# Attention with a sum of tanh over 128 features: the sixteen leftover keys of each image packed into three matmul banks and summed by TensorE, with smaller VectorE steps and longer rests in the side work

## The chip, the cores and the metric

The kernel runs on one core of one Trainium2 chip. The metric is the device time of one execution in microseconds; the number before is the median of three runs. All data are float32.

## The reference

The input is a batch of eight images, 128 channels of 36 x 36 points. Layer 0 is a convolutional attention block (3x3 convolutions for queries, keys and values, softmax attention over 34 x 34 key positions, a tanh, a 1x1 convolution), added to its input. Layer 1 reads each image as 1296 tokens of 128 features. Its attention scores are not a dot product:

```python
def _L1_attn_ref(x, mask, Wq, bq, Wk, bk, w, bw):
    q = jnp.einsum('bld,ed->ble', x, Wq) + bq
    k = jnp.einsum('bld,ed->ble', x, Wk) + bk
    t = jnp.tanh(q[:, :, None, :] + k[:, None, :, :])
    scores = jnp.einsum('bijd,d->bij', t, w) + bw[0]
    attn = jax.nn.softmax(scores, axis=-1)
    return jnp.einsum('bij,bjd->bid', attn, x)
...
t = t + _L1_attn_ref(_ln_t(t), ...)
t = t + _L1_ffn_ref(_ln_t(t), ...)
```

After it comes a layer of 64 experts. A softmax over the 1296 tokens gates each expert; each expert takes its eight best tokens, pools them, and writes its result back to them.

## The kernel before

**How tanh becomes matmuls.** The 128 features are split into 16 groups of five and 8 groups of six. Within a group, the sum of w tanh(q + k) is one fraction: the denominator is a sum over all sign patterns of exp(sign . q) exp(sign . k), and the numerator is the same sum with each pattern weighted by its sum of w. A group of five has 32 patterns and a group of six has 64, so a matmul over 32 or 64 rows makes one group's denominator (or numerator) for 128 keys and 432 queries. The features of the signs lie in NF = 8 blocks of 128 rows: blocks 0 to 3 hold four groups of five each, blocks 4 to 7 two groups of six each. The keys' part is `kf`, the queries' part `qf` (part 0 for denominators, part 1 for numerators).

**Units and slots.** Eight images (b), three chunks of 432 queries (c), and eleven tiles of keys (j): ten of 128 keys and a last one of REM = 16 keys. A unit is one (b, c, j); the last keys stand sixth in a chunk (`order.insert(5, NKT - 1)`). A unit of 128 keys has 12 slots, each with two groups: in turn two slots of fives from one block and one slot of sixes. The unit of the last keys has three slots (`REM_SLOTS`, L61), 2952 slots in all.

**What a slot does** (the loop at L991, in the order of the engines' queues):

```python
            take_turns(p)
            ns = numerators(p)
            denominators(p + LAG)
            terms(p, ns)
            if pending and pending[0][0] <= p:
                exps(p, *pending.popleft()[1:])
            ...
            matmul_turn(p)
            if last:
                pending.append((p + 7, u, sums(u)))
```

`denominators` runs LAG = 3 slots ahead: two matmuls into a PSUM tile `d` of two banks (two such tiles), then ScalarE takes the logarithm into `lq` (L872); every second slot one exponential with scale -1 over two slots turns the logarithms into reciprocals (L875). `numerators` makes two matmuls into two banks `n`, out of a ring of four. `terms` lets VectorE multiply numerators by reciprocals. In slots 2, 5, 8 and 11 (`DVE_PAIRS`) VectorE also adds the products up itself (L892 to L899); in the other eight the products `rp` (three buffers) go to GpSimd, which adds them to `accp` (L908, L910). `sums` (L914) adds the halves on GpSimd, and seven slots later ScalarE takes the exponential (L935) as attention weight `e`.

**The last keys before.** In a slot of the last keys (L853 to L859) four blocks stand side by side, each in 108 columns of a bank, and the four 108-query pieces of the chunk in the four 32-partition strips; the 16 keys are stored twice to fill a strip. A slot has 32 matmuls of 108 columns for the denominators and as many for the numerators. Three logarithms, two exponentials, six multiplications, two GpSimd additions of 864 columns and three more in `sums` follow.

**Side work.** Everything else is written as Python generators in four lanes: first_of_all (query blocks), urgent (the weighted sum `attend`), gates (the experts' gates of the image before), background (all of the next image: `normal`, `conv_keys`, `layer0`, `tokens`, `keys`). A generator says at each yield whether its next part wants matmuls (`matmuls(rest)`) or other engines (`TAKE`, `step(rest)`) and for how many slots it rests. `take_turns` (L958) issues one waiting part of each lane at the start of a slot, ahead of that slot's terms. `matmul_turn` (L963) issues matmuls at its end, with a budget of PACE = 350 columns per slot. The side work uses the same ring of four `n` banks. Engines run their queues in order, so a part that waits holds up whatever stands behind it.

In `tokens` (L539) each image is turned into tokens (tpl), VectorE takes the statistics of eleven tiles (L573, L574), GpSimd raises the variance to -1/2 (`rsqrt`, L221), VectorE normalizes into `xh` out of a second set of transposes (tpn, L593), and a third (tpc) makes `xT`. `keys` (L617) makes the keys' exponentials `ks` and stores them in DRAM (`kd`), from which `prefetch` loads `kf` two units ahead. In `gate_tokens` (L759) ScalarE scales the gates `probs` (L774) and VectorE finds the eight best (L777).

Of the kernel before, what the change touches and what calls it, by code (L numbers as in the profile page):

```python
# [19 lines left out]
CH = 432  # L20
# [37 lines left out]
DVE_PAIRS = (2, 5, 8, 11)  # L58
PACE = 350

REM_SLOTS = [([q + m for m in range(NF // 2)], rows) for q, rows in SLOTS[:3]]  # L61


@with_exitstack
def kernel(
# [55 lines left out]
    with ExitStack() as loop, ExitStack() as score:  # L121
# [34 lines left out]
        def load_x(b):  # L156
# [382 lines left out]
        def tokens(b):  # L539
# [42 lines left out]
            nc.gpsimd.memset(xh[:, :, C : C + 1], 1.0)  # L582
            yield matmuls()
            for g in range(0, NKT, 4):
                tp = aux("tpn")
                some = list(range(g, min(g + 4, NKT)))
                for t in some:
                    o, n = KT[t]
                    turned_to(tp[:n, (t - g) * C : (t - g + 1) * C], r[:, o : o + n], ident)
                yield TAKE  # L590
                for t in some:
                    n = KT[t][1]
                    nc.vector.tensor_scalar(  # L593
                        xh[:n, t, :C], tp[:n, (t - g) * C : (t - g + 1) * C],
                        mv[:n, t, 0:1], rs[:n, t : t + 1], ALU.subtract, ALU.mult,
                    )
                yield matmuls()
# [105 lines left out]
        def gate_logits(b, chunks):  # L703
# [23 lines left out]
            for c in chunks:  # L727
                tp, tt = turned(c, "t2T")
                yield TAKE
                nc.vector.tensor_copy(tt, tp[:, :CH])  # L730
                nc.sync.dma_start(t2d[b][:, c * CH : (c + 1) * CH], tt)
                yield matmuls(1)
                tp = aux("tp3")
                for j in range(TPC):
                    turned_to(tp[:T, j * C : (j + 1) * C], tt[:, j * T : (j + 1) * T], ident)
                yield TAKE
                for j in range(TPC):
                    t = c * TPC + j
                    nc.vector.tensor_scalar(
                        t2[:T, t, :], tp[:T, j * C : (j + 1) * C],  # L740
                        mv[:, t, 0:1], rs[:, t - tiles[0] : t - tiles[0] + 1],
                        ALU.subtract, ALU.mult,
                    )
                yield matmuls(1)
            for c in chunks:
# [13 lines left out]
        def gate_tokens(b):  # L759
# [13 lines left out]
            yield step()  # L773
            nc.scalar.activation(pr, pr, AF.Copy, scale=inv)  # L774
            yield step(2)
            top = small.tile([E, 8], F32, tag="top", name="top")
# [45 lines left out]

        def ends(u, k):

            return k % 2 == 1 or (units[u][2] == NKT - 1 and k == len(REM_SLOTS) - 1)

        def prefetch(u):
# [15 lines left out]
        def products(u, k, part, outs):  # L843
# [3 lines left out]
            if j < NKT - 1:  # L847
# [4 lines left out]
                return  # L852
            blocks, rows = REM_SLOTS[k]  # L853
            for i, q in enumerate(blocks):
                for h in range(2):
                    for s in range(TPC):
                        mm(outs[h][32 * s : 32 * s + 32, i * T : (i + 1) * T], kf[rows[h], q, :32],  # L857
                           qf_of[b, c, q][rows[h], part, s * T : (s + 1) * T],
                           start=True, stop=True)  # L859

        def denominators(p):
# [4 lines left out]
            d = ps_d.tile([128, 2, 512], F32, tag="d", name="d")  # L866
            products(u, k, 0, [d[:, h, :] for h in range(2)])
# [4 lines left out]
            nc.scalar.activation(lq[:, o : o + 2, :], d[:, :, :CH], AF.Ln)  # L872
            if ends(u, k):
                some = lq[:, : o + 2, :]
                nc.scalar.activation(some, some, AF.Exp, scale=-1.0)  # L875

        def numerators(p):
            ns = [ps_n.tile([128, 512], F32, tag="n", name="n") for _ in range(2)]
            products(*slots[p], 1, ns)
            return [ps[:, :CH] for ps in ns]  # L880

        def terms(p, ns):
# [17 lines left out]
            else:  # L900
                rp = rpp.tile([128, 2, CH], F32, tag="rp", name="rp")
                for h in range(2):
                    mult(rp[:, h, :], ns[h], lq[:, o + h, :])  # L903
                if k == 0:
                    live["r"] = rp
# [3 lines left out]
                else:  # L909
                    nc.gpsimd.tensor_add(live["p"], live["p"], rp)  # L910
            if ends(u, k):
                lq_of.pop((u, k // 2))

        def sums(u):  # L914

            s = live.pop("p")
            nc.gpsimd.tensor_add(s[:, 0, :], s[:, 0, :], s[:, 1, :])  # L917
            if units[u][2] < NKT - 1:
                d = live.pop("d")
                nc.gpsimd.tensor_add(d, s[:, 0, :], d)  # L920
                return d
            d = s[:, 0, :T]
            nc.gpsimd.tensor_add(s[:, 0, : 2 * T], s[:, 0, : 2 * T], s[:, 0, 2 * T :])
            nc.gpsimd.tensor_add(d, d, s[:, 0, T : 2 * T])
            return d
# [3 lines left out]
        def exps(p, u, d):  # L929
# [7 lines left out]
            if len(es[b, c]) == NKT:  # L937
                urgent.append(attend(b, c, es.pop((b, c))))

        class Lane(deque):  # L940
# [50 lines left out]
        for p, (u, k) in enumerate(slots):  # L991
# [26 lines left out]
            matmul_turn(p)  # L1018
            if last:
                pending.append((p + 7, u, sums(u)))  # L1020
# [188 lines left out]
```

## Time and profile before

| | |
|---|---|
| median of 3 runs | 6224.16 us (6222.77 to 6229.79) |
| profiled execution | 6231.12 us, span 6229.4 us |
| TensorE matmuls busy | 5995.0 us |
| ScalarE busy | 5348.8 us |
| VectorE busy | 4829.1 us |
| GpSimd busy | 4697.9 us |
| mean granted TensorE clock | 0.970 |

The slot loop runs from 186 us (the first numerator) to 6053 us of the span; ahead of it lie the first image's layer 0 and keys, behind it the experts. Busy shares are averages over stages with different limits, so the stages are read one by one: an ordinary stretch, the last keys, the tokens, the last batch. A matmul's end is modelled, so starts are the safer times. A group's row gives busy time and the mean of one, then the idle time of its engine just ahead of it and what ended that.

### The profile page before, as it was taken

To read this page: it belongs to the slowest core of one execution; us is meant where nothing else is said; L and a number is where in the kernel's file an instruction comes from. 1 tells how busy PE (TensorE), PEld (TensorE's weight loads), DVE (VectorE), ACT (ScalarE), POOL (GpSimd) and SP (SyncE) were. 2 spreads that over 40 slices of the span, in tenths; PEclk is the share of its full clock that TensorE was granted. 3 is DMA by queue.
4 is the path that set the end of the run, shared out by engine and by line. 5 is a ranking of instruction groups with operands and counts; after the bars stand their busy time and mean duration, and the time that the engine had idled before them with its cause. 6 is when DMAs were issued, how large, how long until landed. Compare 5 with 4: busy or idle time off the path is not lost.

```text
span 6229.4 us, 108419 instructions
## 1 busy us (share of the span) xinstructions
PE 5995.0 (96%) x41064; PEld 2940.3 (47%) x41064; DVE 4829.1 (78%) x9595; ACT 5348.8 (86%) x5426; POOL 4697.9 (75%) x2868
## 2 busy tenths in 40 slices
PE   7999999999999999999999999999999999999996
PEld 5454455544554445544445444554445444544443
DVE  3687778877788777887788786887778877788872
ACT  1799998998989989899898998899888998999980
POOL 3678777787778877888787886778777886778870
PEclk9999999999999999999999998999999998999996
DMA  1210021100110001100111001110021000100017
GB/s 43 70 36 24 21 65 38 34 25 28 63 46 23 27 30 65 37 27 23 51 45 41 22 23 59 41 36 22 24 65 48 24 26 27 59 30 28 25 62 267
DMA packets 158891, 272.37 MB, mean 44 GB/s; under 512 B 53856, under 2 KB 83424, under 8 KB 158368
## 3 DMA queue, kind: packets, MB, share of 16 engines
q1 hardware_dynamic: 158368, 265.44, 13.1%
q8 instruction: 323, 5.29, 0.4%
q14 instruction: 200, 1.64, 0.1%
HBM read 200.94 MB, written 64.19 MB: 43 GB/s over the span
## 4 chain that ended last, share of the span: by engine, by line
PE 75%; DVE 9%; ACT 6%; issue 6%; POOL 2%; DMA 1%; SPq 0%; DVEq 0%; POOLq 0%; ACTq 0%
PE n L850 36%; PE d L850 11%; PE pa L240 7%; PE pc L240 5%; ACT lq L872 5%; DVE n L897 3%; PE s L240 3%; PE pk L240 3%; PE pq L240 2%; DVE rp L903 2%; DVE accd L899 1%; PE n L857 1%; PE d L857 1%; POOL accp L910 1%; PE px L240 1%
## 5 line engine op out<-in xcount | busy, mean ns | idle before, releaser
L910 POOL TENSOR_TENSOR accp<-accp,rp 128x864 f32<-128x864 f32 x1464 | 2965.8, 2026 | 1012.3 <-DVE rp L903 948.0
L850 PE MATMUL n<-qf,kf 32*128 32x432 f32 (+1 forms) x11520 | 3280.2, 576 | 65.3 <-DVE xh L593 17.0
L872 ACT ACTIVATE lq<-d 128x864 f32<-128x864 f32 x2952 | 2553.2, 882 | 521.2 <-PE d L850 476.4
L850 PE MATMUL d<-qf,kf 32*128 32x432 f32 (+1 forms) x11520 | 2878.1, 566 | 39.0 <-ACT lq L872 34.7
L903 DVE TENSOR_TENSOR rp<-n,lq 128x432 f32<-128x432 f32 x3984 | 2196.6, 599 | 570.7 <-PE d L850 397.9
L875 ACT ACTIVATE lq<-lq 128x1728 f32<-128x1728 f32 x1488 | 2429.1, 1632 | 47.1
L850 PEld LDWEIGHTS n<-qf,kf 32*128 32x128 f32 (+1 forms) x11520 | 1186.6, 185 | 1609.0 <-DVE rp L903 451.8
L850 PEld LDWEIGHTS d<-qf,kf 32*128 32x128 f32 (+1 forms) x11520 | 1033.3, 187 | 405.5 <-issue 230.9
L897 DVE TENSOR_TENSOR n<-n,lq 128x432 f32<-128x432 f32 x1440 | 811.6, 608 | 264.9 <-PE n L850 229.5
L899 DVE TENSOR_TENSOR accd<-n,accd 128x432 f32<-128x432 f32 x1440 | 866.8, 602 | 24.6
L908 POOL TENSOR_TENSOR accp<-rp 128x864 f32<-128x864 f32 x264 | 534.5, 2025 | 155.9 <-DVE rp L903 153.9
L917 POOL TENSOR_TENSOR accp<-accp 128x432 f32<-128x432 f32 x264 | 291.7, 1105 | 17.6
L648 POOL TENSOR_SCALAR qf<-qf,cs_s 128x432 f32<-128x432 f32 x192 | 261.2, 1366 | 42.2 <-ACT qf L647 42.2
L240 PEld LDWEIGHTS pa<-xh,e 128*108 128x108 f32 x1920 | 224.0, 175 | 131.8 <-DVE rp L903 77.0
L920 POOL TENSOR_TENSOR accd<-accp,accd 128x432 f32<-128x432 f32 x240 | 266.1, 1109 | 23.5 <-DVE accd L899 5.5
L240 PE MATMUL pa<-xh,e 128*108 128x129 f32 x1920 | 263.3, 284 | 10.3 <-DVE accd L899 6.0
L892 DVE TENSOR_TENSOR accd<-n,lq 128x432 f32<-128x432 f32 x240 | 144.7, 603 | 113.4 <-PE n L850 84.0
L240 PE MATMUL s<-q,k 128*116 128x432 f32 x480 | 230.3, 568 | 2.2 <-DVE q L272 1.4
L426 ACT ACTIVATE e<-s 116x432 f32<-116x432 f32 x240 | 125.0, 521 | 118.9 <-PE s L240 118.6
L240 PEld LDWEIGHTS pk<-xT,a_k 128*128 128x128 f32 x1408 | 171.1, 192 | 106.7 <-issue 27.5
L417 POOL TENSOR_TENSOR tot<-tot,e 116x432 f32<-116x432 f32 x192 | 212.2, 1105 | 6.7 <-ACT e L426 4.5
L240 PE MATMUL pa<-e,vw 116*128 116x432 f32 x480 | 206.1, 552 | 2.8 <-DVE accd L899 2.8
(202 smaller groups left out, 3984.5 us busy)
## 6 DMA issues: line engine op xcount, KB each, us to landing
kf<-kd SPq DMA_DIRECT2D x240, 512.0 KB
kd<-ks SPq DMA_DIRECT2D x160, 256.0 KB
w<-in_weight_dram SPq DMA_DIRECT2D x32, 1024.0 KB
wk_t<-wk_t_d SPq DMA_DIRECT2D x7, 768.0 KB
wv_t<-wv_t_d SPq DMA_DIRECT2D x7, 768.0 KB
wq_t<-wq_t_d SPq DMA_DIRECT2D x7, 768.0 KB
x<-in_x_dram SPq DMA_DIRECT2D x8, 648.0 KB
t<-tokd SPq DMA_DIRECT2D x96, 54.0 KB
```

The source lines that it names most:

```text
L240: mm(out, lhsT, rhs, **kw)
L648: nc.gpsimd.tensor_scalar(qf[:, 1, :], qf[:, 0, :], cs_s[:, q : q + 1], None, ALU.mult)
L850: mm(outs[h][:, :CH], kf[rows[h], q, :], qf_of[b, c, q][rows[h], part, :], start=True, stop=True)
L872: nc.scalar.activation(lq[:, o : o + 2, :], d[:, :, :CH], AF.Ln)
L875: nc.scalar.activation(some, some, AF.Exp, scale=-1.0)
L897: mult(ns[h], ns[h], lq[:, o + h, :])
L899: nc.vector.tensor_add(live["d"], ns[h], live["d"])
L903: mult(rp[:, h, :], ns[h], lq[:, o + h, :])
L908: nc.gpsimd.tensor_add(live["p"], live["r"], rp)
L910: nc.gpsimd.tensor_add(live["p"], live["p"], rp)
L917: nc.gpsimd.tensor_add(s[:, 0, :], s[:, 0, :], s[:, 1, :])
L920: nc.gpsimd.tensor_add(d, s[:, 0, :], d)
```

## The change

The last keys now use three full banks: two banks hold the 16 groups of five, one holds the 8 groups of six. A matmul takes half a block (64 rows) of fives or a whole block (128 rows) of sixes and all 432 queries, and writes a strip of 32 partitions: 16 keys of one group and 16 keys of another. That works because `keys` stores the last keys twice, each copy masked to one of the two groups by a column of zeros and ones (`pairs`). The unit has two slots: the first with two banks, the second with one. The products are no longer added on GpSimd. A matmul with a matrix of zeros and ones (`by_key`) adds the rows of the same key over the three banks, in `rem_scores`, and ScalarE takes the exponential out of PSUM.

Besides: PACE is 365 instead of 350; in `tokens` the statistics go two tiles to a step instead of three, the matmuls behind the root rest three slots, and `xh` is made two tiles at a time instead of four; in `gate_logits` the second set of transposes goes two at a time; in `gate_tokens` GpSimd instead of ScalarE scales `probs`, except for the last image, with a rest of three slots instead of two.

```diff
-PACE = 350
-REM_SLOTS = [([q + m for m in range(NF // 2)], rows) for q, rows in SLOTS[:3]]
+PACE = 365
+HALVES = [slice(0, 64), slice(64, 128)]
+REM_BANKS = [[(q + i, rows) for i in range(2) for rows in HALVES] for q in (0, 2)]
+REM_BANKS.append([(NF // 2 + i, slice(0, 128)) for i in range(4)])
+REM_SLOTS = [REM_BANKS[:2], REM_BANKS[2:]]
...
+        pairs = const.tile([128, 2, 2], F32, tag="pairs", name="pairs")
+        nc.gpsimd.memset(pairs, 0.0)
+        for s in range(2):
+            nc.gpsimd.memset(pairs[64 * s : 64 * s + 64, 1, s : s + 1], 1.0)
+            for o in (32 * s, 64 + 32 * s):
+                nc.gpsimd.memset(pairs[o : o + 32, 0, s : s + 1], 1.0)
+        by_key = const.tile([128, 2, REM], F32, tag="by_key", name="by_key")
+        for s in range(2):
+            nc.vector.tensor_reduce(
+                by_key[:, s, :], ident.rearrange("p (b m) -> p m b", m=REM), AX.X, ALU.add
+            )
...
-                if t % 3 == 2:
+                if t % 2 == 1:
                     yield step()
...
-            yield matmuls()
-            for g in range(0, NKT, 4):
+            yield matmuls(3)
+            for g in range(0, NKT, 2):
                 tp = aux("tpn")
-                some = list(range(g, min(g + 4, NKT)))
+                some = list(range(g, min(g + 2, NKT)))
...
-                    nc.sync.dma_start(kd3[:, :, :n], ks[:, :, :n])
                     if n == REM:
-                        nc.sync.dma_start(kd3[:, :, n : 2 * n], ks[:, :, :n])
+                        for x in range(2):
+                            nc.gpsimd.tensor_scalar(
+                                ks[:, :, (x + 1) * n : (x + 2) * n], ks[:, :, :n],
+                                pairs[:, min(q0, 1), x : x + 1], None, ALU.mult,
+                            )
+                        nc.sync.dma_start(kd3[:, :, : 2 * n], ks[:, :, n : 3 * n])
+                    else:
+                        nc.sync.dma_start(kd3, ks)
...
-                tp = aux("tp3")
-                for j in range(TPC):
-                    turned_to(tp[:T, j * C : (j + 1) * C], tt[:, j * T : (j + 1) * T], ident)
-                yield TAKE
-                for j in range(TPC):
...
+                for j0 in range(0, TPC, 2):
+                    tp = aux("tp3")
+                    for j in (j0, j0 + 1):
+                        turned_to(tp[:T, j * C : (j + 1) * C], tt[:, j * T : (j + 1) * T], ident)
+                    yield TAKE
+                    for j in (j0, j0 + 1):
...
-            nc.scalar.activation(pr, pr, AF.Copy, scale=inv)
-            yield step(2)
+            if b == NB - 1:
+                nc.scalar.activation(pr, pr, AF.Copy, scale=inv)
+            else:
+                nc.gpsimd.tensor_scalar(pr, pr, inv, None, ALU.mult)
+            yield step(3)
...
-            blocks, rows = REM_SLOTS[k]
-            for i, q in enumerate(blocks):
-                for h in range(2):
-                    for s in range(TPC):
-                        mm(outs[h][32 * s : 32 * s + 32, i * T : (i + 1) * T], kf[rows[h], q, :32],
-                           qf_of[b, c, q][rows[h], part, s * T : (s + 1) * T],
-                           start=True, stop=True)
+            for out, bank in zip(outs, REM_SLOTS[k]):
+                for i, (q, rows) in enumerate(bank):
+                    mm(out[32 * i : 32 * i + 32, :CH], kf[rows, q, :32],
+                       qf_of[b, c, q][rows, part, :], start=True, stop=True)
...
-                for h in range(2):
-                    mult(rp[:, h, :], ns[h], lq[:, o + h, :])
-                if k == 0:
+                for h, n in enumerate(ns):
+                    mult(rp[:, h, :], n, lq[:, o + h, :])
+                if rem:
+                    live.setdefault("rem", []).extend(rp[:, h, :] for h in range(len(ns)))
+                elif k == 0:
...
+        def rem_scores(p, u, rps):
+            yield matmuls(1)
+            ps = aux("rem")
+            for h, rp in enumerate(rps):
+                for i in range(TPC):
+                    mm(ps[32 * i : 32 * i + 32, :T], by_key.rearrange("p x m -> p (x m)"),
+                       rp[:, i * T : (i + 1) * T], start=(h == 0), stop=(h == len(rps) - 1))
+            behind[0] += 3 * (T + 20)
+            yield TAKE
+            exps(p + 2, u, ps[:, :T])
+            yield matmuls()
...
-            if last:
+            if last and rem:
+                first_of_all.append(rem_scores(p, u, live.pop("rem")))
+            elif last:
                 pending.append((p + 7, u, sums(u)))
```

More of the change, by code (lines that the diff above doesn't have):

```diff
@@ L732, in gate_logits @@
                 yield matmuls(1)
-                tp = aux("tp3")
-                for j in range(TPC):
-                    turned_to(tp[:T, j * C : (j + 1) * C], tt[:, j * T : (j + 1) * T], ident)
-                yield TAKE
-                for j in range(TPC):
[L738 to L744, printed above, removed]
+                for j0 in range(0, TPC, 2):
[4 more added lines that the diff above has]
+                    for j in (j0, j0 + 1):
+                        t = c * TPC + j
+                        nc.vector.tensor_scalar(
+                            t2[:T, t, :], tp[:T, j * C : (j + 1) * C],
+                            mv[:, t, 0:1], rs[:, t - tiles[0] : t - tiles[0] + 1],
+                            ALU.subtract, ALU.mult,
+                        )
+                    yield matmuls()
             for c in chunks:
@@ L821 @@
         kf_of, qf_of, lq_of, live = {}, {}, {}, {}
-        def ends(u, k):
-            return k % 2 == 1 or (units[u][2] == NKT - 1 and k == len(REM_SLOTS) - 1)
         def prefetch(u):
@@ L852, in products, with banks @@
                 return
-            blocks, rows = REM_SLOTS[k]
-            for i, q in enumerate(blocks):
-                for h in range(2):
-                    for s in range(TPC):
-                        mm(outs[h][32 * s : 32 * s + 32, i * T : (i + 1) * T], kf[rows[h], q, :32],
-                           qf_of[b, c, q][rows[h], part, s * T : (s + 1) * T],
-                           start=True, stop=True)
+            for out, bank in zip(outs, REM_SLOTS[k]):
+                for i, (q, rows) in enumerate(bank):
+                    mm(out[32 * i : 32 * i + 32, :CH], kf[rows, q, :32],
+                       qf_of[b, c, q][rows, part, :], start=True, stop=True)
+        def banks(u, k):
+            return 2 if units[u][2] < NKT - 1 else len(REM_SLOTS[k])
         def denominators(p):
@@ L866, in denominators @@
             d = ps_d.tile([128, 2, 512], F32, tag="d", name="d")
-            products(u, k, 0, [d[:, h, :] for h in range(2)])
+            n = banks(u, k)
+            products(u, k, 0, [d[:, h, :] for h in range(n)])
             if k % 2 == 0:
@@ L871, in denominators @@
             o = 2 * (k % 2)
-            nc.scalar.activation(lq[:, o : o + 2, :], d[:, :, :CH], AF.Ln)
-            if ends(u, k):
-                some = lq[:, : o + 2, :]
+            nc.scalar.activation(lq[:, o : o + n, :], d[:, :n, :CH], AF.Ln)
+            if k % 2 == 1:
+                some = lq[:, : o + n, :]
                 nc.scalar.activation(some, some, AF.Exp, scale=-1.0)
         def numerators(p):
-            ns = [ps_n.tile([128, 512], F32, tag="n", name="n") for _ in range(2)]
+            ns = [ps_n.tile([128, 512], F32, tag="n", name="n") for _ in range(banks(*slots[p]))]
             products(*slots[p], 1, ns)
@@ L910, in terms @@
                     nc.gpsimd.tensor_add(live["p"], live["p"], rp)
-            if ends(u, k):
+            if k % 2 == 1:
                 lq_of.pop((u, k // 2))
@@ L917, in sums @@
             nc.gpsimd.tensor_add(s[:, 0, :], s[:, 0, :], s[:, 1, :])
[L918 to L924, printed above, removed]
+            d = live.pop("d")
+            nc.gpsimd.tensor_add(d, s[:, 0, :], d)
             return d
@@ L938, in exps @@
                 urgent.append(attend(b, c, es.pop((b, c))))
+        def rem_scores(p, u, rps):
[8 more added lines that the diff above has]
+            exps(p + 2, u, ps[:, :T])
+            yield matmuls()
         class Lane(deque):
```

## The prediction

> **What bounds the kernel now.** I read the page first (busy shares, slices), then busy time by stage, then the groups kept apart by shape, then the order of time on TensorE and VectorE around the last keys and the tokens.
>
> From the page, the busy shares and the TensorE clock in 40 slices:
>
> ```profile
> PE 5995.0 (96%) x41064; PEld 2940.3 (47%) x41064; DVE 4829.1 (78%) x9595; ACT 5348.8 (86%) x5426; POOL 4697.9 (75%) x2868
> ...
> PEclk9999999999999999999999998999999998999996
> ```
>
> TensorE looks full, but this is an average over stages. Busy time by stage, in the order chunk 1 of batch 1, chunk 2 of batch 1, an ordinary stretch, a stretch of the last batch, two last-key stretches of six slots (three that issue its denominators, three with its numerators), and the tokens stage:
>
> ```profile
> 1163.00:1405.30 242.30, 239.53 (x1629) 111.55 (x1629) 193.65 (x376) 222.00 (x227) 198.72 (x122) 1.00 0.07 23
> 1405.30:1663.50 258.20, 248.90 (x1693) 120.34 (x1692) 196.58 (x392) 230.72 (x240) 192.50 (x116) 0.96 0.14 46
> 1300.00:1340.00 40.00, 39.91 (x195) 17.02 (x195) 31.14 (x59) 36.96 (x41) 33.33 (x21) 1.00 0.08 27
> 5600.00:5640.00 40.00, 38.26 (x209) 17.62 (x210) 30.39 (x59) 38.28 (x40) 36.15 (x22) 1.00 0.06 19
> 1272.91:1287.66 14.75, 14.29 (x416) 7.75 (x414) 10.11 (x20) 12.08 (x12) 11.13 (x7) 1.00 0.12 39
> 2017.18:2035.39 18.21, 17.49 (x416) 9.11 (x414) 10.50 (x20) 11.85 (x12) 11.12 (x7) 0.81 0.10 31
> 1536.00:1563.00 27.00, 22.84 (x100) 10.80 (x99) 21.57 (x61) 18.38 (x19) 16.43 (x11) 0.76 0.13 42
> ```
>
> The columns are length, then PE, PEld, DVE, ACT, POOL, the granted clock, DMA. Three things are to be seen. In ordinary slots TensorE and ScalarE are both above 90%; in the last batch, which has no background, ScalarE is the tighter (38.28 of 40). In the last-key stretches TensorE alone is full and ScalarE has a fifth of its time free. And the clock falls to 0.81 and 0.76 in one last-key stretch and in the tokens stage, which is why chunk 2 takes 258.2 us and chunk 1 only 242.3.
>
> The groups that carry the durations:
>
> ```profile
> L872 ACT ACTIVATE lq<-d 128x864 f32<-128x864 f32 x2952 | 2553.2, 882 | 521.2 <-PE d L850 476.4 <-PE d L857 19.0 <-PE n L850 1.6
> L875 ACT ACTIVATE lq<-lq 128x1728 f32<-128x1728 f32 x1464 | 2406.9, 1644 | 46.4
> L903 DVE TENSOR_TENSOR rp<-n,lq 128x432 f32<-128x432 f32 x3984 | 2196.6, 599 | 570.7 <-PE d L850 397.9 <-ACT lq L875 66.2 <-PE n L857 44.8
> L593 DVE TENSOR_SCALAR xh<-tpn,ln_mv,ln_rs 128x128 f32<-128x128 f32 x80 | 27.4, 403 | 23.2 <-POOL ln_rs L221 20.6 <-PE tpn L244 2.5
> L774 ACT ACTIVATE probs<-probs,ginv 64x1296 f32<-64x1296 f32 x8 | 10.9, 1361 | 0.2 <-DVE ginv L772 0.2
> L782 POOL TENSOR_TENSOR gt<-probs,gt 64x1296 f32<-64x1296 f32 x7 | 20.5, 2933 | 0.0
> ```
>
> And in the order of time: a denominator slot of the last keys, the tokens stage of batch 2, and four matmuls of 128 rows by 32 columns late in the kernel:
>
> ```profile
> 2018.11 1.05 PE L857 MATMUL d<-qf,kf 32*32 32x108 f32 x64
> 2019.09 0.99 PE L850 MATMUL n<-qf,kf 32*128 32x432 f32 x4
> ```
> ```profile
> 1552.88 1.37 DVE L593 TENSOR_SCALAR xh<-tpn,ln_mv,ln_rs 128x128 f32<-128x128 f32 x4 [2.50 <-POOL ln_rs L221]
> ```
> ```profile
> 1554.31 1.14 PE L850 MATMUL n<-qf,kf 32*128 32x432 f32 x3 [2.29 <-DVE xh L593]
> ```
> ```profile
> 6157.36 1.06 PE L1082 MATMUL phid<-w,pooled_s 128*32 128x512 f32 x8 [1.69 <-DMA w<-in_weight_dram]
> 6158.36 1.06 PE L1086 MATMUL phid<-b_s,ident 16*32 16x512 f32 x8
> ```
>
> One f32 matmul leaves two records. The 32 small matmuls of a last-key slot take 0.98 us from start to next start. VectorE stood 2.50 us at the head of its queue for GpSimd's root, and TensorE lost 2.29 us behind it.
>
> **The change, part by part.** My sum is made against the profiled execution (6231.1 us, span 6229.4), which lies 7 us above the median of 6224.2; I subtract the same difference at the end. Anything under 0.2% (12 us) a measurement of this kernel cannot tell from no change.
>
> *Last keys on TensorE.* Removed in each of 24 stretches: 192 matmuls of 108 columns, six slot parts at 0.98 us, 5.9 us. Added: 24 matmuls of 432 columns in six banks, four at a time. For the bank of sixes the nearest row is phid: four of 128x32x512 take 1.00 us, so 432 columns are 0.84 us. The two banks of fives use 64 rows by 32; the trace has no row where both row halves write one bank. Bounds: 0.84 us if all four overlap, 1.68 if the halves take turns. I take 0.88, since the small matmuls above also overlap eight tiles at once. Six banks: 5.3 us. The sum by key adds 12 matmuls of 108 columns (the 32-record pout groups next to phid need 1.01 us for 16 of 128 columns, so 0.65 us). Together 5.9 again: TensorE's own work does not shrink.
>
> *A rule against the change.* The Trainium skill, "TensorEngine Tiling", section "Restrictions and Gotchas", says that different row tiles cannot access the same PSUM bank at the same time. Before, the row halves of L857 write two banks (outs[h]) and reach 0.98 us for 32; the new fives put both halves into one. By the rule four of the six bank passes cost 0.84 us more, 3.4 us a stretch, 81 us in all, and nothing would be won. I go by the row, because the halves write different partitions, and keep the rule as a rival.
>
> *What the stretch saves.* It has five slots for six. In ordinary slots n and d of fives run side by side in 0.93 us, sixes take 1.65, and background costs about 0.6 (350 counted columns, where an s product of 452 takes 0.91 us, less the slots with none). Around the last keys nothing runs side by side: three ordinary n and three d parts cost 2 x (0.93 + 0.93 + 0.82) = 5.4. The stretch 1272.91:1287.66 fits: 5.9 + 5.4 + 6 x 0.6 = 14.9 against 14.75. After: 5.3 + 5.4 + 5 x 0.6 = 13.7, 1.1 less; the 0.6 of background and 0.65 of the sum by key come back in ordinary slots, where TensorE has some slack (1.16 + 0.6 of 1.95 us) and ScalarE is as tight. I count half of the 1.25 as hidden: 0.5 us a stretch, 12 us. The 24 stretches took 386.8 us from first to last numerator start, a mean of 16.1, so 1.35 us above the undisturbed one; that is the clock and its stalls, 33 us in all. With fewer waits half should go: 16 us.
>
> *ScalarE, VectorE, GpSimd.* Per stretch ScalarE loses 3 x 0.88 + 1.64 + 0.92 and gains 0.88 + 0.5 + 1.25, 2.6 us less; VectorE loses three multiplications, 1.8 us; GpSimd loses 6.2 us of additions. TensorE covers all of it except in the last batch, where ScalarE is the bound: 3 x 2.6 = 8, of which I count 5. If ScalarE were the bound everywhere it would be 62.
>
> *Tokens.* Statistics go two tiles to a take (0.8 us for 1.2 to 2.4), the numbers behind the root wait three slots, xh goes two to a take. In the stage shown TensorE stood still 1.17, 0.71 and 2.29 us, 4.2 us; seven such stages are 29 us, and I count 24. The half clock that followed lasted two times 6.83 us in that window (27 us at 0.76 is 6.5 us of clock), worth 6.5 us at TensorE's pace. Here a second rule weighs: "TensorE: Matmul & The Clock Gate", Part 1, wants an idle window of about 3.4 us before the clock halves. By it no gap here is long enough, the clock would stay as it is, and this term is nothing. The trace halved it behind waits of 2.29 and even 0.7 us, so I go by the trace and count half of 7 x 6.5, 23 us. Late next: tpn now takes an n buffer in six slots instead of three.
>
> *Gates.* The scaling of probs (L774, 1.36 us) leaves ScalarE in seven batches; GpSimd takes it at 2.9 us (gt, same shape) to 4.1 us (qf's 1366 ns for 432 columns, tripled). GpSimd's spare sixth covers it, but rp additions queue behind it, and VectorE's MAX8, three slots (5.9 us) later, waits if GpSimd is two additions behind. Gain 10, cost 0 to 14; I take 4. Halved t takes: 2.
>
> *Small things.* The mask of the last keys is four short GpSimd multiplications a batch, at most 0.4 us each by L924's 108 columns, and one DMA fewer from each pair; the stores wait for GpSimd on SP's queue with prefetches behind, which are issued two units (45 us) ahead. If that cover were gone, one prefetch per batch would be late by a GpSimd backlog of some 4 us, 28 in all. The scores wait in an n bank for ScalarE's turn, up to a slot, and numerators queue behind it: I charge 4 us (0 to 15). PACE moves nothing by itself: 366 x 365 and 369 x 350 columns are within 4%, and the built order has the keys of the next batch ending in the last slots both ways.
>
> Sum: 12 + 16 + 5 + 24 + 23 + 4 + 2 - 4 = 82. 6231.1 - 82 = 6149 for a profiled execution; less 7, 6142 for the median.
>
> **The rivals.** *Stalls only move* (20%): clocks stay halved, VectorE waits for GpSimd's scaling instead of the root. Left are 12 + 5 + 24 - 4 = 37, so 6187. For it: the tanh of layer 0 halves the clock too and is untouched. Against: the waits for the root are plainly named.
> *ScalarE was the bound in ordinary slots* (14%): its 62 us and the 10 of the gates count, with tokens and clock: 62 + 10 + 24 + 23 + 16 = 135, so 6089. For it: 36.96 and 38.28 of 40. Against: it is freed where it had slack.
> *Row halves take turns in a bank* (7%): 82 less 81, 6223, no change.
> *All four matmuls of a bank of fives run one after another* (4%): 3 x 0.84 more in four passes, 10 us a stretch, 242 in all, 6384. It turns the change slower from a bank pass of 0.84 + 82/96 = 1.7 us on. For it: the rule above; against: eight tiles at once in L857.
> That the last keys are not done as said is excluded by the built order: 12 bank matmuls for each part and 12 sums a stretch.
>
> **How the numbers follow.** The forecast has 55% (6142, own range 6105 to 6180). Faster: 55 + 20 + 14, less a little for the first rival's edge, 0.88; same 0.07; slower 0.05. Leaving out the last rival and the extremes, the range is 6075 to 6205.
>
> **What would show it.** Right: bank passes of four matmuls at 0.84 to 0.95 us; last-key stretches of five slots near 14 us; waits of TensorE for xh gone; chunk 2 within 8 us of chunk 1; the clock above 0.975. Wrong: passes of 1.7 us or more; MAX8 waiting for GpSimd; the clock still near 0.8 in the tokens stage; or ordinary slots that grew by what the stretches lost.

## The result and the profile after

| | before | after |
|---|---|---|
| median | 6226.45 us (4 runs, 6222.77 to 6229.79) | 6192.11 us (4 runs, 6189.61 to 6194.09) |
| ratio to before, 95% | | 0.9945 (0.9928 to 0.9962) |
| profiled execution, span | 6231.12, 6229.4 us | 6189.61, 6187.9 us |
| mean granted clock | 0.970 | 0.979 |
| slot loop, first to last numerator | 5867.9 us | 5828.0 us |

The changed kernel is faster by 34 us. The forecast was 82 us, with a range from 19 to 149. So the sign is right and the size is less than half. The question for the experiments is where the other 48 us went.

From the page of the changed kernel, the busy shares and the clock in 40 slices:

```profile
PE 5946.4 (96%) x33576; PEld 2834.5 (46%) x33576; DVE 4799.7 (78%) x9525; ACT 5275.0 (85%) x5371; POOL 4584.2 (74%) x2794
...
PEclk9999999999999999999999999999999999999997
```

TensorE has 7488 records fewer and is busy 49 us less; the two slices with an 8 are gone. Busy time by stage, in the order chunk 1 of batch 1 (batches are the images, counted from 0), chunk 2 of batch 1, one last-key stretch of five slots (chunk 1 of batch 3; the mean of all is shorter, 12.87 us), and the tokens stage of batch 2 (length, then PE, PEld, DVE, ACT, POOL, granted clock, DMA):

```profile
1167.80:1415.20 247.40, 244.74 (x1327) 109.77 (x1325) 194.73 (x375) 221.75 (x232) 194.55 (x118) 1.00 0.07 24
1415.20:1662.90 247.70, 239.94 (x1384) 113.81 (x1383) 194.88 (x390) 226.02 (x235) 185.61 (x110) 0.99 0.14 48
2757.46:2772.11 14.65, 14.65 (x86) 5.22 (x85) 9.24 (x17) 9.36 (x10) 8.73 (x6) 1.00 0.12 37
1536.00:1563.00 27.00, 26.04 (x161) 10.77 (x159) 23.77 (x57) 22.12 (x23) 17.98 (x12) 1.00 0.11 41
```

Chunk 2 fell from 258.2 to 247.7 us, and the tokens stage now has TensorE busy 26.04 of 27 us at clock 1.00, where it was 22.84 at 0.76. But chunk 1, which had no such trouble, grew from 242.3 to 247.4 us, with one slot fewer. So the two chunks came together from both sides.

The groups that answer to those of before:

```profile
L898 ACT ACTIVATE lq<-d 128x864 f32<-128x864 f32 x2904 | 2504.8, 882 | 519.5 <-PE d L875 498.0 <-PE d L880 3.5 <-PE n L875 1.0
L929 DVE TENSOR_TENSOR rp<-n,lq 128x432 f32<-128x432 f32 x3912 | 2160.8, 600 | 557.9 <-PE d L875 398.8 <-PE n L875 45.0 <-POOL accp L936 31.4
L611 DVE TENSOR_SCALAR xh<-tpn,ln_mv,ln_rs 128x128 f32<-128x128 f32 x80 | 28.6, 404 | 3.1 <-POOL ln_rs L239 2.3 <-PE tpn L262 0.8
L803 POOL TENSOR_SCALAR probs<-probs,ginv 64x1296 f32<-64x1296 f32 x7 | 24.9, 3557 | 0.0
L875 PE MATMUL n<-qf,kf 64*128 64x432 f32 x3840 | 1126.4, 581 | 23.2 <-ACT e L958 16.0 <-ACT e L444 2.5 <-DVE rp L929 0.3
```

VectorE's idle time behind GpSimd's root fell from 20.6 us to 2.3 (one wait, in the first image, which has no cover). GpSimd scales `probs` in 3.56 us. The last row has something new: the ordinary numerators of sixes stood 16.0 us behind an exponential `e` of L958. That is the exponential of the last keys' scores.

TensorE in the order of time, at the last keys of batch 3, chunk 0:

```profile
2514.05 1.65 PE L880 MATMUL d<-qf,kf 64*32 64x432 f32 x16
2515.64 1.36 PE L258 MATMUL pc<-xwin,wk_t 128*128 128x216 f32 x6
...
2517.85 0.93 PE L880 MATMUL d<-qf,kf 128*32 128x432 f32 x8
2518.71 1.00 PE L875 MATMUL n<-qf,kf 64*128 64x432 f32 x4
...
2529.23 0.76 PE L969 MATMUL rem<-rp,by_key 128*32 128x108 f32 x24
2529.92 0.99 PE L875 MATMUL n<-qf,kf 64*128 64x432 f32 x2
2532.21 1.09 PE L875 MATMUL n<-qf,kf 64*128 64x432 f32 x1 [1.30 <-ACT e L958]
```

From start to next start the two banks of fives (16 records are eight matmuls) take 1.59 us, 0.79 a bank; the bank of sixes takes 0.86, the sum by key 0.69. Then one numerator starts, and its partner only after 1.30 us of waiting. ScalarE at that time:

```profile
2529.49 1.64 ACT L901 ACTIVATE lq<-lq 128x1728 f32<-128x1728 f32 x1
2531.04 0.87 ACT L898 ACTIVATE lq<-d 128x864 f32<-128x864 f32 x1
2531.81 0.34 ACT L958 ACTIVATE e<-rem,eb_s 128x108 f32<-128x108 f32 x1
```

The 0.34 us exponential stands behind 1.64 and 0.87 us of slot work, and the second numerator starts when it is done. Between 2529.92 and 2532.21 TensorE starts nothing else, and VectorE and then ScalarE run dry behind it:

```profile
2534.05 0.62 DVE L919 TENSOR_TENSOR n<-n,lq 128x432 f32<-128x432 f32 x1 [2.27 <-PE n L875]
2535.49 0.89 ACT L898 ACTIVATE lq<-d 128x864 f32<-128x864 f32 x1 [3.34 <-PE d L875]
```

Busy time of the 7 us ahead of the wait and the 7 us behind it, then of the whole unit that follows the last keys:

```profile
2525.00:2532.00 7.00, 5.86 (x56) 2.92 (x52) 4.55 (x9) 6.19 (x7) 4.03 (x3) 1.00 0.45 122
2532.00:2539.00 7.00, 6.79 (x20) 3.87 (x24) 1.58 (x3) 2.69 (x3) 1.09 (x1) 0.52 0.00 0
2527.45:2553.76 26.31, 24.91 (x164) 13.59 (x163) 17.05 (x33) 19.05 (x20) 13.00 (x8) 0.87 0.09 25
```

Right behind the wait the clock is granted at 0.52. TensorE stays "busy" (6.79 of 7) and starts 20 records where it had started 56. This is one of the worst of the 24 places. In all of them the second numerator starts late, 0.90 to 2.29 us behind the first where 0.47 is usual for a slot of sixes, but the clock falls to half behind four of them only.

Added up over all slots (from the starts of the numerators), the 24 last-key stretches fell from 386.8 us to 309.0, which is 78 us. The ordinary slots outside them grew from 1.952 to 1.965 us, 38 us over 2808 slots. The forecast had counted 42 us in the stretches (24 x 1.1, and 16 for the clock), and some 40 us to be saved in the ordinary slots, most of it by the tokens part. So the stretches gave more than was forecast, and the ordinary slots grew where they should have shrunk.

### The profile page after: what moved, and what is told of

Read it like the earlier page. It is cut to its first block, busy times and chain, and to the rows that moved or that the text cites. A ratio compares the mean times of both kernels' runs of the same rounds, so it can differ in the third digit from the quotient of the medians.

```text
span 6187.9 us, 93159 instructions
## 1 busy us (share of the span) xinstructions
PE 5946.4 (96%) x33576; PEld 2834.5 (46%) x33576; DVE 4799.7 (78%) x9525; ACT 5275.0 (85%) x5371; POOL 4584.2 (74%) x2794
## 4 chain that ended last, share of the span: by engine, by line
PE 65%; DVE 11%; POOL 8%; ACT 8%; issue 8%; DMA 1%; SPq 0%; POOLq 0%; DVEq 0%; ACTq 0%
PE n L875 30%; PE d L875 10%; PE pa L258 7%; ACT lq L898 5%; PE pc L258 5%; DVE n L923 4%; POOL accp L938 4%; DVE rp L929 3%; PE s L258 3%; PE pk L258 3%; DVE accd L925 2%; POOL qf L673 1%; POOL accp L936 1%; PE d L880 1%; PE pq L258 1%
## 5 line engine op out<-in xcount | busy, mean ns | idle before, releaser
L938 POOL TENSOR_TENSOR accp<-accp,rp 128x864 f32<-128x864 f32 x1440 | 2915.1, 2024 | 996.5 <-DVE rp L929 943.5
L898 ACT ACTIVATE lq<-d 128x864 f32<-128x864 f32 x2928 | 2517.6, 879 | 555.8 <-PE d L875 498.0
L875 PE MATMUL d<-qf,kf 32*128 32x432 f32 (+1 forms) x11520 | 2907.7, 563 | 46.4 <-ACT lq L898 40.5
L929 DVE TENSOR_TENSOR rp<-n,lq 128x432 f32<-128x432 f32 x3912 | 2160.8, 600 | 557.9 <-PE d L875 398.8
L901 ACT ACTIVATE lq<-lq 128x1728 f32<-128x1728 f32 (+1 forms) x1464 | 2398.2, 1638 | 46.3
L875 PEld LDWEIGHTS d<-qf,kf 32*128 32x128 f32 (+1 forms) x11520 | 1046.9, 186 | 449.8 <-issue 241.7
L936 POOL TENSOR_TENSOR accp<-rp 128x864 f32<-128x864 f32 x240 | 485.2, 2022 | 244.8 <-DVE rp L929 244.7
L945 POOL TENSOR_TENSOR accp<-accp 128x432 f32<-128x432 f32 x240 | 264.7, 1103 | 15.8
```

Of the source, the lines that this page charges most:

```text
L875: mm(outs[h][:, :CH], kf[rows[h], q, :], qf_of[b, c, q][rows[h], part, :], start=True, stop=True)
L898: nc.scalar.activation(lq[:, o : o + n, :], d[:, :n, :CH], AF.Ln)
L929: mult(rp[:, h, :], n, lq[:, o + h, :])
L936: nc.gpsimd.tensor_add(live["p"], live["r"], rp)
```

## The experiments

All ratios below are to the kernel before on the same chip, whose own median lay between 6226 and 6238 us; a ratio is turned into time at 6226 us. B names the theory that the lost time is the wait for the score bank. The rivals were PACE; the scaling of `probs` on GpSimd; and V: VectorE, which now waits with its next product for the sum by key to have read a product buffer.

**1. PACE alone, on the kernel before.**

```diff
-PACE = 350
+PACE = 365
```

> The kernel before with PACE 365 alone; it is the base for the two parts that follow, which need the larger budget. Every theory: within 5 us of before (6226), since the background of an image is the same work and only moves earlier; if the larger budget itself stretches ordinary slots, up to 15 us more.

Measured: 6262.19 us, ratio 1.0052 (1.0039 to 1.0065), 32 us slower. The prediction said that PACE moves nothing by itself; here it does. In the built order of this kernel the next image's keys end in slot 347 of the image's 369, against slot 2 of the next image before. In the last 22 slots of an image the only side work left is then the query blocks of the next chunk. Busy time of eight of them with next to none (slots 349 to 356 of batch 4), in this kernel, and of the same eight slots in the kernel before:

```profile
3881.00:3895.57 14.57, 13.86 (x69) 5.31 (x65) 12.39 (x24) 14.44 (x14) 10.97 (x6) 1.00 0.14 21
```
```profile
3858.61:3875.53 16.92, 16.88 (x99) 8.80 (x98) 11.81 (x22) 16.60 (x20) 12.15 (x6) 1.00 0.17 63
```

A slot without side work takes 1.82 us here, with it 2.11. It is shorter, but no shorter than ScalarE allows (14.44 of 14.57 us busy), so only part of the time that the side work took earlier is won back. That this makes up the 32 us is argued, not measured here; experiment 4 tests it. In the changed kernel itself the longer rests push the same keys back to slot 367 of 366, so there are no empty slots.

**2. One part alone, at PACE 365.** The tokens part on the kernel before, and the new last keys alone (with tokens, gates and the halved transposes as before):

```diff
-PACE = 350
+PACE = 365
...
-                if t % 3 == 2:
+                if t % 2 == 1:
...
-            yield matmuls()
-            for g in range(0, NKT, 4):
+            yield matmuls(3)
+            for g in range(0, NKT, 2):
...
```

> The kernel before with PACE 365 and only the tokens part (statistics two tiles to a step, rest of three slots behind the root, xh two tiles at a time). Theory 1, the gain of 34 us is the clock of the tokens stage and its waits: 25 to 40 us less than before, half-clock time in the loop down from 236 us to 150 or less. Theory 2, the gain is that of the last keys: 0 to 10 us less.

> The kernel before with PACE 365 and only the new last keys (three banks, two slots, sum by key on TensorE). Theory 1: within 10 us of before, because TensorE gives back in the ordinary slots (sums by key 0.69 us, background of the slot that is gone, waits for the score bank) what the stretch saves. Theory 2: 25 to 40 us less, with no half clock left in the last-key stretches (87 us before).

Measured: tokens 6225.27 us, ratio 0.9992 (0.9983 to 1.0002); keys 6235.61, ratio 1.0008 (1.0000 to 1.0016). Each part by itself brings nothing at this PACE. The next image's keys end in slots 354 of 369 and 348 of 366, so both carry slots with little side work, and the question had to be asked again at a smaller budget.

**3. The scaling of `probs` back on ScalarE, in the changed kernel.**

```diff
-            if b == NB - 1:
-                nc.scalar.activation(pr, pr, AF.Copy, scale=inv)
-            else:
-                nc.gpsimd.tensor_scalar(pr, pr, inv, None, ALU.mult)
-            yield step(3)
+            nc.scalar.activation(pr, pr, AF.Copy, scale=inv)
+            yield step(2)
```

> The changed kernel with the scaling of probs back on ScalarE and a rest of two slots. If GpSimd's 3.55 us scaling (seven times) holds up additions and VectorE behind them: 5 to 15 us less than the changed kernel (6192). If it is covered: within 4 us; if ScalarE is tight there: up to 10 us more.

Measured: 6203.01 us, ratio 0.9955 (0.9943 to 0.9966), against 0.9945 with the scaling on GpSimd. That would be a gain of about 6 us for the move, but the intervals overlap. GpSimd's 3.56 us are not where the 48 us went.

**4. The same two parts at PACE 354,** where the keys end in slots 368 of 366 and 373 of 369. Both kernels differ from those of 2 in that number alone.

> Only the new last keys, with PACE 354, so that the next image's keys end in the last slots of an image, as before and as in the changed kernel (at PACE 365 they ended 18 slots early). Theory P, the cost of PACE 365 alone (32 us) is the slots left without side work at an image's end, where ScalarE is the bound: 6200 to 6212, 25 to 35 us less than keys_365. Rival Q, a fuller slot costs more in itself: half of that, 6218 to 6225.

> Only the tokens part, with PACE 354, keys again ending in the last slots (11 slots early at 365). Theory P: 6195 to 6210, 15 to 30 us less than tokens_365. Rival Q: 6212 to 6220. If both parts come out near 25 us less than before, their sum is more than the 34 us of the whole change, and what is lost lies in the budget that the rests need together.

Measured: keys 6209.71 us, ratio 0.9965 (0.9953 to 0.9978), so 22 us; tokens 6203.80, ratio 0.9955 (0.9940 to 0.9970), so 28 us. Both lie where theory P put them, and both are faster than rival Q allowed. That speaks for the slots left without side work as what the larger budget costs. From the waits of TensorE (us in total, times, longest), first of the last keys alone, then of the tokens part alone, then of the kernel before:

```profile
PE n L871 <- DVE xh L611: 18.5, 7, 3.6
PE n L871 <- ACT e L954: 17.1, 16, 1.3
```
```profile
PE d L850 <- ACT lq L872: 38.8, 63, 3.7
PE n L850 <- DVE accd L899: 14.0, 35, 1.6
```
```profile
PE n L850 <- DVE xh L593: 17.0, 7, 2.6
PE n L850 <- DVE accd L899: 8.6, 20, 0.6
```

The wait for `e` belongs to the new last keys. In the tokens part the wait for `xh` (17.0 us in 7 waits before) is gone, and that for VectorE's `accd` has grown from 8.6 to 14.0 us.

**5. The bank not taken at all.** In the changed kernel the sum by key and its bank are left out, and with them the last keys' scores; the columns stay in the budget.

```diff
-            ps = aux("rem")
-            for h, rp in enumerate(rps):
-                for i in range(TPC):
-                    mm(ps[32 * i : 32 * i + 32, :T], by_key.rearrange("p x m -> p (x m)"),
-                       rp[:, i * T : (i + 1) * T], start=(h == 0), stop=(h == len(rps) - 1))
...
-            exps(p + 2, u, ps[:, :T])
+            exps(p + 2, u, rps[0][:, :T])
```

> The changed kernel without the twelve matmuls of the sum by key and their bank; the budget still counts them, so the order of all other work is the same. The exponential reads a product tile instead, so the last keys' scores are left out. If the sum by key costs its own time and the waits that the trace shows for it (16.6 us of TensorE, 16 for the bank, 16 of VectorE for the product buffer): 25 to 40 us less than the changed kernel (6192). If TensorE's slack covers it: within 8 us.

Measured: 6152.24 us, ratio 0.9876 (0.9857 to 0.9895), 77 us faster than before. The removed matmuls are 0.69 us of TensorE 24 times, 17 us; the gain over the changed kernel is 43 us by the two ratios. So the bank and what waits for it cost more than its matmuls. Both B and V allow that, since VectorE's wait for the sum's reads went too.

**6. The first product of the last keys in another pool.** In the changed kernel, the product tile of the first of the two slots comes from the pool that ordinary units use for `accp`, so that VectorE's next product needs no buffer that the sum by key still reads.

```diff
-                rp = rpp.tile([128, 2, CH], F32, tag="rp", name="rp")
+                if rem and k == 0:
+                    rp = acc.tile([128, 2, CH], F32, tag="accp", name="accp")
+                else:
+                    rp = rpp.tile([128, 2, CH], F32, tag="rp", name="rp")
```

> The changed kernel with the first product tile of the last keys in the accumulator's free second buffer, so that VectorE's second product tile of the next unit no longer waits for the sum by key (15.9 us in 24 waits). If that wait is on the path: 8 to 16 us less than the changed kernel; if VectorE has slack there: within 4 us.

Measured: 6150.75 us, ratio 0.9872 (0.9855 to 0.9889): 80 us faster than before. This kernel is aimed at V's wait, and by itself the gain looks like V. But the bank numbers of the built program show that it changes the order of the banks too. In the changed kernel the bank of the scores is handed to the second numerator of the next slot, two bank requests later, all 24 times; here the next request for that bank comes four later. The same place in this kernel, TensorE:

```profile
2510.44 0.58 PE L972 MATMUL rem<-accp,by_key 128*32 128x108 f32 x16
2510.84 0.37 PE L972 MATMUL rem<-rp,by_key 128*32 128x108 f32 x8
2511.14 1.32 PE L875 MATMUL n<-qf,kf 64*128 64x432 f32 x4
2511.97 1.22 PE L875 MATMUL d<-qf,kf 64*128 64x432 f32 x4
```

Both numerators (x4) stand in one row now, without a wait. ScalarE reads the scores at 2513.03, as late as before, and it no longer matters. The unit behind the last keys, and 7 us of it, in this kernel:

```profile
2508.66:2530.01 21.35, 21.27 (x164) 12.24 (x163) 16.91 (x33) 18.78 (x20) 13.00 (x8) 1.00 0.12 32
2508.00:2515.00 7.00, 6.95 (x66) 4.18 (x69) 4.61 (x9) 6.20 (x8) 3.34 (x2) 1.00 0.38 113
```

The unit with the same 164 matmul records takes 21.35 us at clock 1.00 in place of 26.31 at 0.87. Over all 24 such units the mean fell from 24.07 to 22.19 us.

**7. Telling the bank from the buffer.** The changed kernel again beside three others. In the first the sum by key stays, in its bank and with VectorE's wait for its reads; only the exponential reads a product tile instead of the score bank, which leaves the last keys' scores out.

```diff
-            exps(p + 2, u, ps[:, :T])
+            exps(p + 2, u, rps[0][:, :T])
```

> The changed kernel unaltered, on the same chip as the three runs that follow. Every theory: a ratio of 0.9945 to before, as in its own runs.

> The changed kernel with its sum by key left in place, but the exponential reads a product tile in SBUF instead of the score bank, so nobody reads the bank (the last keys' scores are left out). VectorE still waits for the sum with its next product tile, and the next slot's second numerator still takes the score bank. Theory B, the bank is the cause (numerators wait in it for ScalarE's exponential, 16 us in 16 waits, and the clock halves after it): ratio 0.986 to 0.989, as without the sums. Theory V, VectorE's wait for the product buffer is the cause: 0.993 to 0.995, as the changed kernel.

Measured: the changed kernel 6187.16 us, ratio 0.9919 (0.9901 to 0.9937); with the exponential off the bank 6149.43, ratio 0.9859 (0.9841 to 0.9876). On one chip that is 38 us for taking ScalarE's read away from the bank. Who waited for the scores' bank and the sum, in the changed kernel and then in this one:

```profile
  PEld n L875: 33.1, 30
  PE n L875: 16.0, 16
  DVE rp L929: 15.9, 24
```
```profile
  DVE rp L929: 20.3, 24
```

VectorE's wait is still there, all 24 times and even longer (20.3 us), and the lost time is gone all the same. V is out; B holds. TensorE here, around the sum by key:

```profile
2519.53 0.76 PE L969 MATMUL rem<-rp,by_key 128*32 128x108 f32 x24
2520.23 1.15 PE L875 MATMUL n<-qf,kf 64*128 64x432 f32 x4
```

The starts of the numerators show where the time went. In the third slot of the 24 units behind the last keys (us over all 24):

| | changed | version of 6 | scores_sbuf |
|---|---|---|---|
| the slot | 95.6 | 51.5 | 51.6 |
| of it, first to second numerator | 39.1 | 11.2 | 11.2 |
| of it, at half clock | 17.7 | 0 | 0 |

**8. The other two of that set:** the last keys alone with the product tile of 6, and the version of 6 with the sum by key one slot later.

```diff
 def rem_scores(p, u, rps):
-            yield matmuls(1)
+            yield matmuls(2)
```

> Only the new last keys, PACE 354, and the first product tile in the accumulator's free buffer, by which the score bank also comes round four numerators later instead of two. If that one wait is what the last keys lose, and if the parts add: 30 to 45 us less than keys_354 (6210), a ratio near 0.990. If it needs the tokens part too: within 15 us of keys_354.

> The changed kernel with the first product tile in the accumulator's free buffer and the sum by key one slot later still, with the score bank coming round five numerators later. Theory B: no cost, within 6 us of the kernel without the delay (6151), as no numerator queues behind ScalarE's turn. Theory V: VectorE's third product tile of the next unit now waits for the later sum (its buffer is the second product tile's): 5 to 20 us more.

Measured: last keys alone 6177.70 us, ratio 0.9904 (0.9884 to 0.9924), 60 us against the 22 of keys_354: again 38 us for the bank, and the wait for `e` is gone from TensorE's waits (in six of the 24 places the second numerator waits 1.34 us for VectorE instead). With the sum one slot later 6151.52 us, ratio 0.9866 (0.9848 to 0.9883), the same as 6: with the bank coming round five requests later, a later sum cost nothing. The version of 6 beats both kernels.

## Why the prediction came out half right

Of the five signs of "right", two held as stated: no matmul of the slot loop waits for `xh`, and the clock is at 0.979. Two were passed on the good side: bank passes of 0.79 and 0.86 us where 0.84 to 0.95 was given, stretches of 12.87 us in the mean for "near 14". The fifth, chunk 2 within 0.3 us of chunk 1, came true for two reasons of which only one was forecast: chunk 2 fell by 10.5 us and chunk 1 rose by 5.1. And one sign of "wrong" held too: the ordinary slots grew, by half of what the stretches lost.

**The step that failed** is the one under small things: "The scores wait in an n bank for ScalarE's turn, up to a slot, and numerators queue behind it: I charge 4 us (0 to 15)." The mechanism was named and its price was more than nine times too low: 38 us, measured in experiment 7. With 38 in place of 4 the sum would have been 48 us. The waits that the profile names are only 16.0 us in 16 places, because it counts a wait from the modelled end of the first numerator. By the starts, the second numerator came 28 us later in all (39.1 less 11.2), in 24 places. Behind four of them the clock halved: 17.7 us of these slots are at half clock, some 9 us of TensorE's work. Nearly all of the cost sits in this one place: the third slot of the 240 ordinary units took 620.9 us in the changed kernel and 574.7 in the version of 6, 46 us less, and 44 of these belong to the 24 units right behind the last keys.

The wait is not the whole growth of the ordinary slots. Without it they are at 1.949 us, against 1.952 before, but not by the same slots. The 24 units behind the last keys took 575.3 us before, 577.8 in the changed kernel and 532.5 without the wait: there it hid what the tokens part had saved. Chunk 1, over the eight images, took 1921.7 us before, 1951.4 in the changed kernel and still 1945.8 without the wait. It holds more side work: counted from the traces, all matmuls but numerators and denominators have 293 thousand columns there, against 271 before, and the sums by key are only 10 of these 22. What moved the rest into chunk 1 was not tried apart. So it is luck that the version of 6, with 80 us, lands so near the forecast of 82: its stretches gave 76 us where 42 were counted, its ordinary slots 7 where some 40 were. What the prediction should have asked is which tile gets that bank next: in the built program it is the very next slot's second numerator, and the reader of the bank stands behind 2.5 us of ScalarE work (1.64 + 0.87).

**Last keys, forecast 12 + 16 + 5 = 33 us; measured 60 with the bank's wait taken out.** TensorE's own work came out as worked: bank passes of 0.79 and 0.86 us for 0.88 and 0.84, the sum by key 0.69 for 0.65. The stretch took 12.87 us where "near 14" was expected. The clock's term was too small: the old stretches held 87 us at half clock, the new ones none, some 43 us of work where I counted half of a 33 us excess. What came back in the ordinary slots was near the forecast: in the last keys alone with the tile of 6 the stretches lost 76 us and the ordinary slots gained 21, where half of 24 x 1.25 us, 15, was expected.

**Tokens, forecast 24 + 23 = 47 us; measured 28 (19 to 37).** The stage itself did what was forecast: with the tokens part alone the units behind the last keys, where the stage lies, fell from 575.3 to 530.1 us, and their time at half clock from 80.5 to 8.5 us. The wait for `xh` went too, though it was only 17.0 us in 7 waits; I took 4.2 us from one window, with gaps in it that `xh` didn't cause, and multiplied by seven. But outside these units the ordinary slots grew by 27 us while the stretches lost 15. Of the growth, 5.4 us are new waits for `accd`; the rest is not explained. That is the first rival ("stalls only move") in part. One reading was wrong as well: the last-key stretch at 0.81 lies in chunk 1 of batch 2, so it is no reason for the 258.2 us of batch 1's chunk 2.

**Gates, forecast 4 us; measured about 6,** not resolved. The scaling took 3.56 us, inside the 2.9 to 4.1 given, and no MAX8 waited for it.

**PACE "moves nothing by itself"** is wrong as a sentence on the budget: alone it costs 32 us, and both parts alone are 23 to 27 us worse at 365 than at 354. The slot in which the keys end was read for the two whole kernels only, where it hardly moves. Whether the changed kernel would gain from a smaller budget was not run.

**The rivals.** Row halves of a bank do not take turns: the bank of fives takes 0.79 us, so what the Trainium skill's "TensorEngine Tiling", section "Restrictions and Gotchas", says against two row tiles in one bank is not what this chip shows for strips of different partitions. The last rival (6384 us) fell with it. ScalarE as the bound of ordinary slots (6089 us) found no support: ScalarE is 74 us less busy, and without the bank's wait the ordinary slots are where they were on average, 1.949 us. The rule of the Trainium skill's "TensorE: Matmul & The Clock Gate", Part 1, about an idle window of some 3.4 us would have put the tokens' and the bank's clock at nothing. Here the clock halved behind waits of 1.30 us (2.29 from start to start), in four of six places alike, so going by the trace was right, and the same reading ought to have been applied to the bank.

**What stays open.** The parts measured apart add up to 60 + 28 + 6 = 94 us, less 38 for the bank, 56; the whole brought 34 us in the first measurement and 50 in the second (6187.16 against 6238.06, intervals that just overlap). The remaining 6 to 22 us may be the budget or the parts' overlap. No run tells them apart, nor why the clock halves behind one such wait and not behind another like it.

## What to carry to other kernels

When a step takes one more buffer from a ring that the main loop also uses, work out which instruction gets that buffer next and what stands before its reader on the reader's queue. Price the wait by how much later the waiter starts, in every place, and by what the clock does behind it, not by the idle time that the profile names. If the next user is close, change the order of requests (here one tile from another pool moved the bank two requests on and was worth 36 to 45 us of 6190) before making any engine faster. And test a part of a change with the pacing it would have by itself: the tokens part showed 28 us at one budget and nothing at another.

## What the runs showed of the hardware that was not expected

- In chunk 0 of batches 1 to 6 the second numerator started 2.28 to 2.29 us behind the first, of which the profile names up to 1.30 us as a wait. In four of these six places the clock was then granted at half for 3.41 or 6.83 us; in two it stayed at 1.00. Without the wait (version of 6) it stayed at 1.00 in all six units.
- Four matmuls of 64 rows by 32 columns and 432 columns in float32, two row halves and four column strips into one PSUM bank, took 0.79 us (mean of a pair, the same in all 48 pairs of the profile), less than four of 128 rows by 32 in the bank of sixes (0.86).
- A buffer's wait on VectorE of 20.3 us in 24 places cost nothing that can be measured (ratio 0.9859 with it, 0.9872 and 0.9866 in the two kernels without it), and one on TensorE, named as 16.0 us in 16 places, cost 38.
